# Running sums of a chunked scan: from a product with ones to rows in device memory read back by all partitions

## The chip, the cores and the metric

The kernel runs on one core of a Trainium2 chip. The metric is device time in microseconds. TensorE (PE), VectorE (DVE), ScalarE (ACT), GpSimd (POOL) and SyncE (SP) each work through a queue of their own, in order; "PEld" is PE's loading of weights, which overlaps its matmuls. SP here only issues DMA transfers.

## What the reference computes

Two layers on x of 2 batches, 512 tokens, 256 features, all in float32. Layer 0 is a Mamba-2 block (a chunked selective scan) whose result is multiplied by the silu of a mixture of 8 experts (2 of 8 per token). Layer 1 is attention with 32 heads over 8 key heads, multiplied by the silu of a layer with signs for weights. What matters here is the scan of layer 0:

```python
log_a = A_c * dt_c
cum_log_a = jnp.cumsum(log_a, axis=2)
log_diff = cum_log_a[:, :, :, None, :] - cum_log_a[:, :, None, :, :]
L = jnp.exp(jnp.where(causal, log_diff, -jnp.inf))
...
decay_to_end = jnp.exp(chunk_log_decay[:, :, None, :] - cum_log_a)
decay_from_start = jnp.exp(cum_log_a).reshape(batch, n_chunks, Q, G, Hg)
```

The running sum of the log decays is needed twice in each difference: as a number per token on the partitions, and as a row along the free dimension that is the same on all partitions.

## The kernel before

The scan is cut into 8 tiles of 128 tokens (t = 0 to 7; four per batch, i0 = 0 to 3) with 4 heads each. For all tiles at once `running_sums` makes `cum`, tokens on partitions, by a product of the triangle `upper` with the log decays `la` (L456), and DVE copies it out of PSUM (L458).

The sums along the free dimension are made tile by tile. `spread` (L466) has DVE multiply the triangle with the tile's log decays, giving `rl` of 128x512 (L470). `decays` (L474) has PE multiply ones with `rl` (L481): every partition then holds all running sums of the tile, 4 heads by 128, in one PSUM bank. From there ACT takes the exponential `ec` (L483), and DVE takes the four differences `L` (L490) and `dte` (L493). PE also turns the tile's inputs (L487, four transposes), which DVE scales to `xdt` (L497). `weighed`, `outputs` and `passed` finish the tile later; they use `ec`, `L`, `xdt`.

Around the scan stand the experts. One expert is `expert_turned` (PE transposes, L606, and DVE's copy to `xgT`, L608), three calls of `expert_hidden` (PE products at L624, ACT's silu at L633, DVE's multiplication at L636 to L641), and `expert_end` (PE at L649, ACT's scaling at L586, POOL's scatter at L587). Rows that overflow an expert go through `rests`: POOL gathers their weights as "piece" tiles (L575), and PE multiplies by them at L719 and L751. The order of all this is written out by hand from L771 to L1084 under a manual schedule: each engine, SP included, gets its instructions in the order of these lines.

SP's queue in this stretch holds the experts' weights: after each `expert_end` come `last_weights_of` (`wp`, 768 KB, L377, which must wait until PE has ended the expert) and `weights_of` (`w`, 1024 and 384 KB, L370 and L371). The part of the order around the second batch's first tile reads:

```python
        expert_end(3)
        last_weights_of(4)
        weights_of(5)
        convolved(1, 3)
        spread(1, 0)
        expert_hidden(4, 2)
        decays(1, 0)
        expert_turned(5)
```

The tag `rl` has two buffers, so `rl` of tile t uses again the buffer of tile t - 2. PSUM has two groups of four banks, "A" for the experts and "B" for the scan.

Of the kernel before, what the change touches and what calls it, by code (L numbers as in the profile page):

```python
# [8 lines left out]
F32 = mybir.dt.float32  # L9
AF = mybir.ActivationFunctionType  # L10
ALU = mybir.AluOpType
AX = mybir.AxisListType

P = 128
B, T, C = 2, 512, 256
NT = B * T // P
TPB = T // P
KC = C // P
DI, NH = 512, 4
# [32 lines left out]
def fused_kernel(  # L52
# [16 lines left out]
    nc = tc.nc  # L69
    V, S, G, PE = nc.vector, nc.scalar, nc.gpsimd, nc.tensor  # L70
# [9 lines left out]
    dram = ctx.enter_context(tc.tile_pool(name="dram", bufs=1, space=bass.MemoryType.DRAM))  # L80
# [7 lines left out]
    def bank_b():  # L88
        return psum.tile([P, 512], F32, tag="B", name="bank_b")
# [4 lines left out]
    def bank(width=512):  # L94

        if not later:
            return bank_b()
        i = turns[0] % 8
        turns[0] += 1
        written[i] = max(written[i], width)  # L100
        return later[i]
# [35 lines left out]
    ones = const.tile([P, P], F32, tag="ones", name="ones")  # L137
    G.memset(ones, 1.0)

    upper = const.tile([P, P], F32, tag="upper", name="upper")  # L140
# [40 lines left out]
           allow_small_or_imprecise_dtypes=True)  # L181
    rows = dram.tile([B * T, C], F32, tag="rows", name="rows")
    chosen = dram.tile([2 * B * T, C], F32, tag="chosen", name="chosen")

    first = const.tile([P, NT, E], F32, tag="first", name="first")
    for e in range(E):
# [99 lines left out]
    def narrow(weights, source):  # L286

        ps = bank_b()
        for g in range(GROUPS):
            for k in range(KC):  # L290
                PE.matmul(ps[g * QUARTER : (g + 1) * QUARTER, : 2 * P], lhsT=weights(k),
                          rhs=source(g, k), start=(k == 0), stop=(k == KC - 1))
        return ps
# [56 lines left out]
    def wide(name, t):  # L350
        return mw.tile([P, NH, P], F32, tag=name, name=f"{name}{t}")

    def lent(tag, name, *shape):

        n = 1
        for d in shape:
            n *= d
        flat = mw.tile([P, NH, P], F32, tag=tag, name=name).rearrange("p h n -> p (h n)")[:, :n]
        if len(shape) == 1:
            return flat  # L360
        names = "abc"[: len(shape)]
        return flat.rearrange(f"p ({' '.join(names)}) -> p {' '.join(names)}",
                              **dict(zip(names, shape)))
# [59 lines left out]
    la = mem.tile([P, NT, NH], F32, tag="la", name="la")  # L423
# [29 lines left out]
    def running_sums():  # L453
# [3 lines left out]
                  start=True, stop=True)  # L457
        V.tensor_copy(cum.rearrange("p t h -> p (t h)"), ps[:, : NT * NH])  # L458

    def heads(ap):  # L460
        return ap.rearrange("p (h n) -> p h n", h=NH)


    states, parts = [None] * B, {}

    def spread(b, i0):  # L466

        t = b * TPB + i0
        rl = wide("rl", t)
        V.tensor_tensor(rl, upper.unsqueeze(1).to_broadcast([P, NH, P]),  # L470
                        la[:, t, :].unsqueeze(2).to_broadcast([P, NH, P]), ALU.mult)
        parts[t] = rl

    def decays(b, i0):  # L474

        t = b * TPB + i0
        ti = slice(i0 * P, (i0 + 1) * P)

        cps = bank_b()
        cumb = heads(cps)  # L480
        PE.matmul(cps, lhsT=ones, rhs=parts[t].rearrange("p h n -> p (h n)"), start=True, stop=True)  # L481
        ec = wide("ec", t)
        S.activation(ec, cumb, AF.Exp)  # L483

        xps = bank_b()
        for h in range(NH):
            PE.transpose(xps[:, h * P : (h + 1) * P], ssmT[b][:, h, ti], ident)  # L487
        L = wide("L", t)
        for h in range(NH):
            V.scalar_tensor_tensor(L[:, h, :], cumb[:, h, :], cum[:, t, h : h + 1], negm,  # L490
                                   ALU.subtract, ALU.add)
        dte = mw.tile([P, NH], F32, tag="dte", name=f"dte{t}")
        V.tensor_tensor(dte, cumb[:, :, P - 1], cum[:, t, :], ALU.subtract)  # L493
        S.activation(L, L, AF.Exp)
        S.activation(dte, dte, AF.Exp)
        xdt = wide("xdt", t)
        V.tensor_tensor(xdt, heads(xps), dt3[:, t, :].unsqueeze(2).to_broadcast([P, NH, P]),  # L497
                        ALU.mult)
        parts[t] = ec, L, xdt, dte
# [18 lines left out]
    def outputs(b, i0):  # L518

        t = b * TPB + i0  # L520
        ec, L, xdt, cs, xe = parts[t]
        state = states[b]
        if xe is not None:
            sps = bank_b()
            PE.matmul(sps, lhsT=Btok[:, t, :], rhs=xe.rearrange("p h n -> p (h n)"),
                      start=True, stop=True)
            new = mw.tile([P, NH, P], F32, tag=f"state{b}", name=f"state{t}")
            if state is None:
                V.tensor_copy(new, heads(sps))
            else:  # L530
                for h in range(NH):
                    V.scalar_tensor_tensor(new[:, h, :], state[:, h, :], ec[:, h, P - 1 : P],
                                           heads(sps)[:, h, :], ALU.mult, ALU.add)
            states[b] = new
        yps = bank_b()
        for h in range(NH):
            y = yps[:, h * P : (h + 1) * P]
            PE.matmul(y, lhsT=xdt[:, h, :], rhs=L[:, h, :], start=True, stop=state is None)
            if state is not None:
                PE.matmul(y, lhsT=state[:, h, :], rhs=cs[:, h, :], start=False, stop=True)  # L540
        parts[t] = yps
# [229 lines left out]
    with tc.manual_schedule():  # L771

        ps = bank_b()
# [11 lines left out]
        for t in range(TPB + 1, NT):  # L785
# [16 lines left out]
        ps = narrow(lambda k: gw[:, k, :],  # L802
                    lambda g, k: xT[:, k, g * 2 * P : (g + 1) * 2 * P])
# [14 lines left out]
        ps = narrow(lambda k: w_in[:, k, o_dt - DI : o_dt - DI + QUARTER],  # L818
                    lambda g, k: hT[g // 2][:, k, g % 2 * 2 * P : (g % 2 + 1) * 2 * P])
# [8 lines left out]
        ps = bank_b()  # L828
        PE.matmul(ps[:, : counted[1]], lhsT=upper, rhs=both[:, 1:].rearrange("p t e -> p (t e)"),
                  start=True, stop=False)  # L830
        PE.matmul(ps[:, : counted[1]], lhsT=ones,
                  rhs=sums[0][:, 3 : 4 + NT].rearrange("p t e -> p (t e)"),
                  start=False, stop=True)
# [67 lines left out]
        ps = bank_b()  # L901
        for t in range(NT):
            for n in range(2):
                PE.matmul(ps[n * HALF : (n + 1) * HALF, :P], lhsT=vals[n][:, t, :],
                          rhs=ohs[n, t // TPB][:, t % TPB, :], start=(t == 0), stop=(t == NT - 1))
# [6 lines left out]
        ps = bank_b()  # L912
# [21 lines left out]
        expert_turned(0)  # L934
        expert_slots(1)
        spread(0, 0)
        gates(0, (3,))

# [22 lines left out]
        next(few)  # L961
        expert_hidden(1, 0)
        decays(0, 0)
        spread(0, 1)
        expert_end(0)
        last_weights_of(1)
        weights_of(2)
        weighed(0, 0)
        decays(0, 1)
        expert_hidden(1, 2)  # L970
        expert_turned(2)
        expert_slots(3)
        weighed(0, 1)
        within(0, 0)
        spread(0, 2)
        expert_hidden(1, 4)
        expert_hidden(2, 0)
        within(0, 1)
        decays(0, 2)
        expert_end(1)  # L980
        last_weights_of(2)
# [439 lines left out]
    with tc.manual_schedule():  # L1421
        prev = done = None
        for n, (b, c) in enumerate(work):
# [35 lines left out]
            if done is not None and done[1] == PAIRS - 1:  # L1459
                kept(*done)  # L1460
                done = None
                for i in range(TPB):
                    ps = bank(C)
# [15 lines left out]
        for i in range(2, TPB):  # L1479
            ps = bank(C)  # L1480
# [89 lines left out]
```

## Time and profile before

| | us |
|---|---|
| median of 3 runs | 630.01 (629.48 to 631.99) |
| the profiled execution | 630.42 |
| its span | 627.7 |
| scan and experts, within the span | about 39 to 235 |
| layer 1, mostly attention | about 235 to 627.7 |

The granted clock of TensorE was 0.997 of full speed in the profiled execution. The page of the profile lists for each engine its busy time, the span in 40 equal slices (15.7 us each; a digit is tenths of busy time), the DMA queues, the chain of work that ended last, and the costliest groups of instructions. A timeline lists, for one engine, start, duration, line, operation, output and inputs, count, and in brackets the idle time ahead of it with what ended it. Windows list the busy time of each engine in each stretch, with the number of instructions, then the granted clock, the share of the 16 DMA engines and GB/s.

### The profile page before, as it was taken

What the parts mean: (1) busy time and instruction counts of PE and PEld (TensorE: products, weight loads), DVE (VectorE), ACT (ScalarE), POOL (GpSimd) and SP (SyncE); (2) the same over time, 40 slices, a digit from 0 to 9 for tenths busy, and PEclk for the clock granted to TensorE, in tenths of its full rate; (3) what the DMA queues carried; (4) which work ended last, traced back from release to release, by engine and by line L of the source; (5) the groups of instructions that cost most, each with busy time, mean ns of one, the idle gap of its engine ahead of it and who ended that gap; (6) DMA issues with size and microseconds to landing.
All of it is one profiled execution on the core that took longest, in us unless ns stands there. A gap on an engine that the chain in (4) does not pass through costs nothing.

```text
span 627.7 us, 11001 instructions
## 1 busy us (share of the span) xinstructions
PE 602.3 (96%) x3847; PEld 410.7 (65%) x3847; DVE 424.9 (68%) x1349; ACT 352.4 (56%) x913; POOL 279.5 (45%) x312
## 2 busy tenths in 40 slices
PE   8989999999998988899889999999999999999997
PEld 6458888777766855365455565666866566666676
DVE  7687764464444238799997789986159888898411
ACT  3533333133331432879788677887048999999610
POOL 3021421364663131575635546565025776666700
PEclk9999999999999999999999999999999999999999
DMA  7810641675865253000000000400000000000000
GB/s 224 280 34 17 235 159 35 223 228 185 288 199 186 72 180 137 2 2 2 1 2 2 1 1 2 135 2 2 18 17 2 2 2 1 3 2 1 2 8 26
DMA packets 24988, 45.74 MB, mean 73 GB/s; under 512 B 2621, under 2 KB 12607, under 8 KB 24928
## 3 DMA queue, kind: packets, MB, share of 16 engines
q1 hardware_dynamic: 19840, 30.71, 14.3%
q0 software_dynamic: 4512, 13.77, 7.1%
q8 instruction: 31, 0.51, 0.3%
q10 hardware_dynamic: 576, 0.52, 0.2%
q14 instruction: 29, 0.24, 0.1%
HBM read 40.80 MB, written 4.33 MB: 72 GB/s over the span
## 4 chain that ended last, share of the span: by engine, by line
PE 46%; DVE 15%; ACT 3%; issue 2%; POOL 2%; ACTq 0%; DVEq 0%; POOLq 0%
PE bank L1302 9%; PE bank L1294 8%; PE bank L1175 7%; PE bank L1243 7%; PE bank L1282 7%; DVE pr L1256 5%; PE bank_a L649 2%; ACT pr L1262 2%; PE bank L1192 1%; POOL pr L1270 1%; DVE sw_q L1165 1%; PE bank_a L260 1%; PE bank_a L624 1%; DVE q L1166 1%; PE bank L1154 1%
## 5 line engine op out<-in xcount | busy, mean ns | idle before, releaser
L1270 POOL TENSOR_SCALAR pr<-pr,den 128x128 f32<-128x128 f32 (+2 forms) x192 | 193.5, 1024 | 146.4 <-DVE den L1435 146.4
L1262 ACT ACTIVATE pr<-pr,nmax 128x128 f32<-128x128 f32 (+3 forms) x256 | 142.2, 562 | 44.4 <-DVE nmax L1256 43.6
L1256 DVE CUSTOM_DVE_ANT_0 pr<-bank,cmask 128x128 f32<-128x128 f32 (+3 forms) x256 | 109.7, 484 | 12.7 <-PE bank L1243 9.2
L1283 ACT COPY pt<-bank 128x384 f32<-128x384 f32 (+1 forms) x192 | 82.4, 526 | 12.6 <-PE bank L1282 12.6
L1282 PEld LDWEIGHTS bank<-ident,pr 128*128 128x128 f32 x640 | 71.6, 141 | 21.6 <-issue 14.4
L1282 PE MATMUL bank<-ident,pr 128*128 128x128 f32 x640 | 75.6, 273 | 4.0 <-DVE oT L1419 3.5
L624 PE MATMUL bank_a<-xgT,w 128*128 128x256 f32 x352 | 79.5, 379 | 0.0
L1294 PE MATMUL bank<-pt,v 128*64 128x384 f32 (+3 forms) x512 | 77.0, 439 | 1.4 <-ACT pt L1283 1.4
L1243 PE MATMUL bank<-kT,q 64*64 64x128 f32 (+7 forms) x1024 | 69.9, 410 | 2.5 <-ACT v L1194 2.5
L624 PEld LDWEIGHTS bank_a<-xgT,w 128*128 128x128 f32 x352 | 65.6, 190 | 9.2 <-issue 1.0
L1294 PEld LDWEIGHTS bank<-pt,v 128*64 128x64 f32 x512 | 35.6, 136 | 45.5 <-issue 22.2
L1175 PE MATMUL bank<-x1T,w_q 128*128 128x512 f32 x124 | 61.5, 618 | 0.0
L1302 PE MATMUL bank<-w_o,oT 128*128 128x256 f32 x256 | 56.1, 380 | 0.6 <-DVE oT L1416 0.6
L1302 PEld LDWEIGHTS bank<-w_o,oT 128*128 128x128 f32 x256 | 48.3, 190 | 7.7 <-DVE oT L1416 0.8
L1262 ACT ACTIVATION_READ_ACCUMULATOR pr<-pr,nmax 128x1 f32 x256 | 50.3, 197 | 0.0
L1243 PEld LDWEIGHTS bank<-kT,q 64*64 64x64 f32 x1024 | 38.0, 133 | 16.2 <-issue 5.1
L575 POOL DMA_INDIRECT piece<-in_moe,wrow x36 | 37.4, 1040 | 21.7 <-issue 9.5
L1175 PEld LDWEIGHTS bank<-x1T,w_q 128*128 128x128 f32 x124 | 21.0, 189 | 37.0 <-issue 27.0
L587 POOL DMA_INDIRECT chosen<-o,dest x16 | 16.3, 1016 | 63.9 <-ACT o L586 37.2
L649 PE MATMUL bank_a<-wp,hid 128*128 128x256 f32 x192 | 43.1, 380 | 0.4 <-PEq L1072 0.3
L575 POOL DMA_INDIRECT xg<-rows,tok x16 | 17.0, 1065 | 54.2 <-DVE res L924 31.5
L649 PEld LDWEIGHTS bank_a<-wp,hid 128*128 128x128 f32 x192 | 35.9, 190 | 6.3 <-issue 1.7
(277 smaller groups left out, 793.7 us busy)
## 6 DMA issues: line engine op xcount, KB each, us to landing
w<-in_moe SPq DMA_DIRECT2D x8, 1024.0 KB, 11.8
wp<-in_moe SPq DMA_DIRECT2D x8, 768.0 KB, 4.2
w<-in_moe SPq DMA_DIRECT2D x8, 384.0 KB, 8.7
w_q<-in_wq SPq DMA_DIRECT2D x2, 1024.0 KB
w_o<-in_wo SPq DMA_DIRECT2D x2, 1024.0 KB
rows<-xn SPq DMA_DIRECT2D x4, 256.0 KB, 2.2
xn<-chosen SPq DMA_DIRECT2D x4, 256.0 KB, 2.6
y<-chosen SPq DMA_DIRECT2D x4, 256.0 KB, 3.8
```

What stands on the lines that cost most here:

```text
L575: G.indirect_dma_start(out=buf, out_offset=None, in_=src[:, :], in_offset=bass.IndirectOffsetOnAxis(ap=at, axis=0), bounds_check=src.shape ...
L624: PE.matmul(ps[:, i * OWN : (i + 1) * OWN], lhsT=w[:, a : a + P], rhs=xgT[:, k * OWN : (k + 1) * OWN], start=(k == 0), stop=(k == KC - 1))
L649: PE.matmul(ps[:, :C], lhsT=hid[j // 2][:, a : a + P], rhs=wp[:, j * C : (j + 1) * C], start=(j == 0), stop=(j == 5))
L1175: PE.matmul(ps, lhsT=w[:, k, n * P : (n + 1) * P], rhs=x1T[:, k, batch(b)], start=(k == 0), stop=(k == KC - 1))
L1243: PE.matmul(pss[hh][to, a : a + full], lhsT=q[half, n * HD : (n + 1) * HD], rhs=kT[b][half, m, :full], start=True, stop=True)
L1256: V.tensor_tensor_reduce(w["pr"][hh][:, span(i)], w["ps"][i][hh], cmask[:, i & 1, T - (i + 1) * P :], -1.0, 3.0e38, ALU.add, ALU.min, w["n ...
L1262: S.activation(x, x, AF.Exp, scale=-1.0, bias=w["nmax"][hh][:, i : i + 1], accum_out=sum_of(w, i, hh))
L1270: eng.tensor_scalar(x, x, sum_of(w, i, hh), None, ALU.mult)
L1282: PE.transpose(ps[:, col : col + P], pr[hh][:, at : at + P], ident)
L1283: S.copy(pts[hh][:, bank_at[n] : bank_at[n] + widths[n]], ps[:, : widths[n]])
L1294: PE.matmul(pv[hh * HD : (hh + 1) * HD, j * P :], lhsT=v_sb[b][:, j, g * HD : (g + 1) * HD], rhs=pts[hh][:, at : at + w], start=(j == 0), ...
L1302: PE.matmul(ps[:, :C], lhsT=oTs[b][:, c, i * P : (i + 1) * P], rhs=made["w_o"][c // 8][:, c % 8, :], start=(c == 0), stop=(c == PAIRS - 1))
```

## The change

The sums by row are made once for all tiles, by a second product with the operands exchanged (32 rows, one for each tile and head, by 128 tokens), copied out of the same PSUM bank by DVE, and written to device memory as `cum_rows` (16 KB). `spread` is no longer DVE's work: it is a DMA on SP that reads the tile's four rows (2 KB) to all 128 partitions (256 KB in SBUF). `decays` uses that tile in place of the PSUM bank. The places of the calls in the order stay as they were. In after.py the new product is L461, its copy L464, the write L465, the loads L477, the exponential `ec` L489 and the differences `L` L496.

```diff
+    cum_rows = dram.tile([NT * NH, P], F32, tag="cum_rows", name="cum_rows")
...
+        PE.matmul(ps[: NT * NH, P : 2 * P], lhsT=la.rearrange("p t h -> p (t h)"), rhs=upper,
+                  start=True, stop=True)
+        by_row = lent("yg", "by_row", P)[: NT * NH]
+        V.tensor_copy(by_row, ps[: NT * NH, P : 2 * P])
+        nc.sync.dma_start(cum_rows[:, :], by_row)
...
     def spread(b, i0):
 
         t = b * TPB + i0
-        rl = wide("rl", t)
-        V.tensor_tensor(rl, upper.unsqueeze(1).to_broadcast([P, NH, P]),
-                        la[:, t, :].unsqueeze(2).to_broadcast([P, NH, P]), ALU.mult)
-        parts[t] = rl
+        cumb = wide("rl", t)
+        nc.sync.dma_start(cumb.rearrange("p h n -> p (h n)"),
+                          cum_rows[t * NH : (t + 1) * NH, :].rearrange("a n -> (a n)")
+                          .partition_broadcast(P))
+        parts[t] = cumb
...
     def decays(b, i0):
...
-        cps = bank_b()
-        cumb = heads(cps)
-        PE.matmul(cps, lhsT=ones, rhs=parts[t].rearrange("p h n -> p (h n)"), start=True, stop=True)
+        cumb = parts[t]
         ec = wide("ec", t)
         S.activation(ec, cumb, AF.Exp)
```

## The prediction, made before the changed kernel had run

> **What bounds the kernel now.** I read the page first: TensorE (PE) is busy 96% of the span, the granted clock is full in every slice, and no other engine passes 68%. Then the slices. The scan and the experts that stand around it lie between about 39 and 235 us, where the DMA row is busy too.
>
> ```profile
> PE 602.3 (96%) x3847; PEld 410.7 (65%) x3847; DVE 424.9 (68%) x1349; ACT 352.4 (56%) x913; POOL 279.5 (45%) x312
> ...
> DMA  7810641675865253000000000400000000000000
> ```
>
> Then the same stretch in windows of 1 us. From 60 to 174 us PE never idles (the sum for 84 to 108 us is 24.00 of 24). So time taken off PE's queue is gained, and a wait that reaches PE is lost, unless something else was already late at the next meeting point. That something is the gather of "piece" tiles by GpSimd (POOL), below.
>
> **What is removed.** The product at L481, its operand at L470 (VectorE, DVE, 0.68 us, eight times). The row of L481 by line, and the place of its first pair in PE's timeline:
>
> ```profile
> L481 PE MATMUL bank_b<-rl,ones x16: 592/592/697, 57.5 to 208.8; 128*128 128x512 f32 x16
> ...
> 57.48 1.02 PE L481 MATMUL bank_b<-rl,ones 128*128 128x512 f32 x2
> 58.34 0.60 PE L487 MATMUL bank_b<-ident,ssmT 128*128 128x128 f32 x4
> ```
>
> Matmuls overlap, so I don't take 592 ns but the distance to the next start: 58.34 - 57.48 = 0.86 us for a pair. The eight pairs read 0.86, 0.86, 0.86, 0.85, 0.86, 0.96, 0.96, 0.86: 7.07 us. Ahead of the seventh pair PE also idles 0.97 us for L470 (it starts at 176.55); that wait goes, and the transposes behind need only old data. Together **-8.04**. The DVE time saved (5.5 us) is worth nothing by itself: PE, not DVE, is the queue without gaps. ScalarE (ACT) and DVE also stop taking turns on the bank of L481 (DVE waited 17.3 us for L483, six times), off PE's path as well; so is what reading SBUF instead of PSUM does to their 0.34 and 0.60 us.
>
> **What is added at about 40 us.** A second product (after.py L461) of 128 columns in the bank that holds the first. In the built program's list of waits it holds a wait of its own for DVE, for the count that the copy of the first product (L458) reaches. That copy is queued on DVE behind a whole convolution (timelines of PE, then DVE, of before):
>
> ```profile
> 39.45 0.38 PE L456 MATMUL bank_b<-la,upper 128*128 128x32 f32 x2 [1.66 <-DVE la L449]
> 39.67 1.96 PE L260 MATMUL bank_a<-hT,w_z 128*128 128x512 f32 x4
> ...
> 39.80 2.33 DVE L402 SCALAR_TENSOR_TENSOR cv<-pad,sm,cv 128x512 f32<-128x512 f32 x3
> 42.04 0.18 DVE L458 COPY cum<-bank_b 128x32 f32<-128x32 f32 x1
> ```
>
> PE now goes on at 39.67. After the change it stands until 42.22, plus 0.14 from DVE's end to PE's start (as from la, 39.12 + 0.19, to 39.45), plus 0.22 for the product (the distance L456 to L260): 42.58, 2.91 us later. Behind it in PE's queue are two gate projections and the transposes of the first expert's tokens; the latter now wait for a gather and take 0.87 us (41.47 to 42.34) instead of 0.44, so 0.43 is absorbed. **+2.48**. Bounds: 0 if the wait were already met, which the times exclude unless DVE is 2.5 us earlier; 2.9 if nothing is absorbed. The second copy (L464) and xgT behind it on DVE stay ahead of PE: xgT would end near 45.6, PE needs it at 46.5.
>
> On this wait the Trainium skill, "PSUM — Partial Sum Buffer", section "PSUM bank collisions raise a hardware error", says that two engines must not touch one bank and quadrant at once, whatever the columns. By it the wait can't be left out and PE pays the 2.48; a rule by bytes alone would give 0 here, as the two products use different columns.
>
> **The write and the eight loads.** The 16 KB write leaves SyncE (SP) near 43 us. SP's writes of now, rows<-xn and out_x<-y, land 2.2 and 1.7 us after issue. Loads 0 and 1 go right behind, by about 48 us, and are needed from 59.6 us (L483): hidden. The others stand on SP in program order behind weights, whose issue waits for PE to end an expert (L649). What counts is the time from that issue to the use:
>
> - Load 2 (SP near 65.7): DMA is saturated until 73.6, so landing near 74.5; needed near 80. Hidden.
> - Load 3 (near 88.3): saturated until 95; landing near 96.4; ACT reaches its use at 97.5. Hidden by 1 us; if late, ACT and DVE have some 10 us before PE needs them.
> - Load 5 goes with load 4 and is needed at 160; load 6 (near 159) lands near 168.5, needed at 176; load 7 (near 185) lands near 193, needed at 208. Hidden.
> - **Load 4** (near 138.6) is not.
>
> ```profile
> 138.05 0.51 SPq L371 DMA_DIRECT2D w<-in_moe  x1
> ...
> w<-in_moe SPq DMA_DIRECT2D x1, 384.0 KB, 8.7
> ...
> 145.00:146.00 1.00, 1.00 (x12) 0.26 (x8) 0.12 (x1) 0.83 (x2) 0.00 (x0) 1.00 0.87 291
> 146.00:147.00 1.00, 1.00 (x11) 0.37 (x4) 0.72 (x2) 0.15 (x1) 0.00 (x0) 1.00 0.14 50
> ```
>
> The first two rows are SP's issue of the last weights ahead of it and their landing: 138.05 + 8.7 = 146.75. The window rows end in DMA share and GB/s; they show the transfers ending there. At the 393 GB/s of 143 to 145 us 256 KB more takes 0.65-0.7: 147.4. The use is L490 on DVE, now at 142.05:
>
> ```profile
> 142.05 1.12 DVE L490 SCALAR_TENSOR_TENSOR L<-bank_b,cum,negm 128x128 f32<-128x128 f32 x4 [0.73 <-ACT ec L483]
> 143.10 0.15 DVE L493 TENSOR_TENSOR dte<-bank_b,cum 128x4 f32<-128x4 f32 x1
> 143.17 0.68 DVE L497 TENSOR_TENSOR xdt<-bank_b,dt 128x512 f32<-128x512 f32 x1
> 143.76 0.68 DVE L608 COPY xgT<-bank_a 128x512 f32<-128x512 f32 x1
> ...
> 146.96 3.62 PE L624 MATMUL bank_a<-xgT,w 128*128 128x256 f32 x16
> ```
>
> Behind L490 on DVE is xgT of expert 5 (L608), and PE's products of that expert wait for it. xgT starts 1.71 us after L490, so 149.11, ends 149.8, PE starts near 149.95. Without the wait PE would be there at 146.96 - 0.86 = 146.10. **+3.85**. ACT's silu behind its own wait (L483) comes back by 151 and stays ahead of PE. Bounds: 0 if the load overtakes the weights; above, the slowest 256 KB rows of the page take 3.8 us from issue to landing (y<-chosen), which behind the queue makes +7.0. I take 3.85, the rate of the queue it stands in, as the nearest row.
>
> The Trainium skill, "DMA: Bandwidth & Descriptors", section "Anatomy of one DMA — SWDGE (gpsimd) path", gives 2.0 us plus bytes over 436 GB/s for one transfer on the other path, an estimate of 2.6 us here. Paid in full behind the weights it would make this wait 5.8 instead of 3.85 and the forecast 631.4; no run here shows it.
>
> **Where the gain meets another wait.** Pieces 4 and 5 are gathered by POOL from 160.30 to 170.88, counted from the end of expert 4, and PE's L719 at 173.59 already takes some 0.5 us more than its 384 columns need (1.99 us against 1.92 for 512). The 0.96 of the sixth pair lies between: PE arrives earlier and waits longer. **+0.96** (bounds 0 and 0.96). Likewise the last piece:
>
> ```profile
> 200.47 0.62 PE L751 MATMUL bank_b<-piece,hrT 128*32 128x256 f32 x2 [0.80 <-DMA piece<-in_moe,wrow]
> 201.80 1.05 PE L751 MATMUL bank_b<-piece,hrT 128*32 128x256 f32 x10 [0.72 <-DMA piece<-in_moe,wrow]
> ```
>
> Its gather follows a scatter on POOL that took 7.0 us (185.79 to 192.79; 3.2 at 155.76) while DMA was full. The weights come 1.9 us earlier against it, load 7 adds 0.65. I take **+0.2**; bounds -1.5 (the waits vanish) and +1.93 (all of the seventh pair is given back).
>
> **Sum:** -8.04 + 2.48 + 3.85 + 0.96 + 0.2 = -0.55. The profiled execution took 630.42 (span 627.7 and 2.7 around it), so 629.9; against the median 630.01, **629.5**. After 235 us nothing changes but the start.
>
> **Rivals.** (1) Load 4 isn't late: the DMA engines might serve it between packets of the weights. Against it: the last weights land just as the transfers end, so the queue is served in order. Then 3.85 more goes: 625.6. (2) Slower: the load itself is slow, because 128 readers ask for the same 2 KB. Load 4 then holds DVE, and PE behind it, for each us more. It ends slower by 0.5% (3.15 us) once the transfer takes 0.65 + 3.7 = 4.35 us (60 GB/s); at 49 GB/s, an eighth of the queue's rate, 5.3 us, +4.7: 634.1. For it: no row shows a load of one row by all partitions. Against it: rows of 2 KB run at 390 GB/s here. (3) The products stay in some form: the built program has none of L481's, so no chance.
>
> **Numbers.** Forecast 0.56 (its own range 627.5 to 632.5), rival 1 0.14, rival 2 0.30, which takes in other late loads. About 0.5% (3.15 us) is what a measurement of this kernel can tell from none: faster 0.14, within 0.56, slower 0.30. Range 625.5 to 634.5: rival 1, the bounds above (629.5 + 3.15 + 1.7 = 634.35) and the near part of rival 2.
>
> **What would show it.** Right: a PE wait for DVE (cum) of about 2.7 us near 40; DVE waiting at the fifth L (after.py L496) some 5 us for the load; PE waiting near 4 us for xgT behind it; L719 and L751 waiting longer for pieces. Wrong: no gap ahead of expert 5; loads 2, 3, 6 late as well; or landings 4 us and more behind the weights.

## The result, and the profile after

The changed kernel takes 636.52 us (median of 4 runs, 634.79 to 637.58); before, beside it, 629.80 (629.48 to 631.99). The ratio is 1.0082, 95% interval 1.0058 to 1.0106: slower by 0.8%, where 629.5 and no difference were forecast. The profiled execution took 636.41 us with a span of 634.5, 6.8 us longer than the span of before.

The page of the changed kernel, its rows of PE's busy time and of the granted clock:

```profile
PE 601.8 (95%) x3833; PEld 410.1 (65%) x3833; DVE 419.9 (66%) x1342; ACT 352.9 (56%) x913; POOL 278.1 (44%) x312
...
PEclk9979999998999998999999999999999999999999
```

PE runs 14 matmuls fewer and is busy almost as long (601.8 beside 602.3). The clock row says why: it is no longer full in the third, the tenth and the sixteenth slice (32 to 48, 143 to 159 and 238 to 254 us). The first two are the places of the two waits that the forecast counted. The third, at half from 248.6 to 255.4, lies around a wait of 3.60 us ahead of the transposes of xn (249.85). It adds nothing that is seen in the total: from the decays of (1,3) to the end both kernels take as long (418.3 and 418.4 us). PE's timeline at the first place:

```profile
39.32 0.38 PE L457 MATMUL bank_b<-la,upper 128*128 128x32 f32 x2 [1.66 <-DVE la L450]
42.15 0.63 PE L461 MATMUL bank_b<-upper,la 128*32 128x128 f32 x2 [2.45 <-DVE cum L459]
42.72 3.78 PE L261 MATMUL bank_a<-hT,w_z 128*128 128x512 f32 x4
46.29 1.05 PE L612 MATMUL bank_a<-ident,xg 128*128 128x128 f32 x4
47.15 1.92 PE L261 MATMUL bank_a<-hT,w_z 128*128 128x512 f32 x4
```

The wait is the forecast one, in place and length: the second product (L461) stands 2.45 us for DVE's copy and starts at 42.15. But what follows is slow: the gate projection (L261) takes 3.57 us to the next start and the transposes 0.86; the same projection at 47.15, once the clock is back, takes 1.75. The windows give the reason, here and for the second place further down (length, busy time of PE, PEld, DVE, ACT and POOL, then **PEclk, the granted clock**, DMA share, GB/s):

```profile
40.00:41.00 1.00, 0.00 (x0) 0.00 (x0) 0.96 (x2) 0.00 (x0) 0.00 (x0) 0.69 0.32 90
...
42.00:43.00 1.00, 0.85 (x3) 0.47 (x4) 0.27 (x2) 0.97 (x2) 0.00 (x0) 0.50 0.00 0
...
46.00:47.00 1.00, 1.00 (x5) 0.71 (x4) 0.00 (x0) 0.46 (x1) 0.00 (x0) 0.50 0.87 211
47.00:48.00 1.00, 1.00 (x4) 0.57 (x3) 0.62 (x2) 0.13 (x1) 0.59 (x1) 0.90 0.65 240
...
153.00:154.00 1.00, 1.00 (x4) 0.82 (x3) 0.04 (x1) 0.99 (x3) 0.47 (x1) 0.51 0.64 172
...
156.00:157.00 1.00, 1.00 (x5) 0.84 (x4) 0.04 (x1) 0.60 (x1) 0.00 (x0) 0.78 0.00 0
```

While PE stands, the clock falls to 0.50 (at 40.4), and it comes back only at 47.2: PE works 5.1 us at half speed after its wait. The first products of the first expert start at 48.90 instead of 44.05: 4.85 us lost. The two rows of before with which the two places are compared, from PE's timeline:

```profile
44.05 6.21 PE L624 MATMUL bank_a<-xgT,w 128*128 128x256 f32 x28
...
150.42 1.02 PE L525 MATMUL bank_b<-xe,Btok 128*128 128x512 f32 x2
```

The second place of the changed kernel, in the timelines of DVE, then PE:

```profile
150.13 1.14 DVE L496 SCALAR_TENSOR_TENSOR L<-rl,cum,negm 128x128 f32<-128x128 f32 x4 [6.46 <-DMA rl<-cum_rows]
...
151.89 0.68 DVE L614 COPY xgT<-bank_a 128x512 f32<-128x512 f32 x1
```
```profile
148.12 0.49 PE L513 MATMUL bank_b<-BC 128*128 128x128 f32 x2
152.62 5.41 PE L630 MATMUL bank_a<-xgT,w 128*128 128x256 f32 x16 [4.01 <-DVE xgT L614]
157.86 1.02 PE L531 MATMUL bank_b<-xe,Btok 128*128 128x512 f32 x2
```

This is the forecast chain link by link: load 4 holds DVE at the fifth L, xgT of expert 5 stands behind it, PE waits 4.01 us. PE was 1.48 us late at L513 (148.12 against 146.64) and is 5.66 late at L630. Then its 16 matmuls take 5.24 us to the next start; before they took 3.46 (146.96 to 150.42). The clock is 0.50 from 153.0 to 156.4, and PE leaves 7.44 us late.

Loads 0 and 1 show what a load costs by itself. They are what the DMA columns of the windows at 46 and 47 us above hold (211 and 240 GB/s); the window before them has 70 GB/s, the one behind them 4. Both, 512 KB, move between 45.5 and 48 us: about 1.25 us each. That is twice the 0.65 that the forecast took from the rate of the weights, and far below the 4.35 from which rival 2 would have been slower by 0.5%.

### The profile page after: what moved, and what is told of

It is laid out like the page before. It is cut to its first block, busy times and chain, and to the rows that moved or that the text cites. A ratio compares the mean times of both kernels' runs of the same rounds, so it can differ in the third digit from the quotient of the medians.

```text
span 634.5 us, 10977 instructions
## 1 busy us (share of the span) xinstructions
PE 601.8 (95%) x3833; PEld 410.1 (65%) x3833; DVE 419.9 (66%) x1342; ACT 352.9 (56%) x913; POOL 278.1 (44%) x312
## 4 chain that ended last, share of the span: by engine, by line
PE 51%; DVE 11%; ACT 2%; issue 1%; POOL 1%; DVEq 0%; POOLq 0%
PE bank L1300 10%; PE bank L1308 9%; PE bank L1181 8%; PE bank L1249 8%; PE bank L1288 8%; DVE pr L1262 4%; PE bank_a L655 2%; PE bank L1198 1%; POOL pr L1276 1%; PE bank_a L261 1%; PE bank L1160 1%; PE bank_a L630 1%; DVE sw_q L1171 1%; PE bank_b L1181 1%; DVE q L1172 1%
## 5 line engine op out<-in xcount | busy, mean ns | idle before, releaser
L630 PE MATMUL bank_a<-xgT,w 128*128 128x256 f32 x352 | 81.7, 386 | 4.8 <-DVE xgT L614 4.0
L630 PEld LDWEIGHTS bank_a<-xgT,w 128*128 128x128 f32 x352 | 66.7, 193 | 15.3 <-DVE xgT L614 4.2
L1300 PEld LDWEIGHTS bank<-pt,v 128*64 128x64 f32 x512 | 35.4, 136 | 45.7 <-issue 22.5
```

Of the source, the lines that this page charges most:

```text
L630: PE.matmul(ps[:, i * OWN : (i + 1) * OWN], lhsT=w[:, a : a + P], rhs=xgT[:, k * OWN : (k + 1) * OWN], start=(k == 0), stop=(k == KC - 1))
L1300: PE.matmul(pv[hh * HD : (hh + 1) * HD, j * P :], lhsT=v_sb[b][:, j, g * HD : (g + 1) * HD], rhs=pts[hh][:, at : at + w], start=(j == 0), ...
```

## The experiments

The table follows PE by the start of the transposes (bank_b<-ident,ssmT) in the decays of four chunks, and by the span, in the profiled execution of each kernel. The ratio is that of all its runs to the runs of before on the same chip.

| kernel | (0,0) | (1,0) | (1,1) | (1,3) | span | ratio, 95% interval |
|---|---|---|---|---|---|---|
| before | 58.34 | 141.22 | 160.26 | 209.27 | 627.7 | 1 |
| after | 62.29 | 142.71 | 166.74 | 216.18 | 634.5 | 1.0082 [1.0058, 1.0106] |
| e1_own_bank | 57.35 | 137.81 | 160.82 | 210.96 | 629.1 | 1.0030 [1.0007, 1.0054] |
| e2_early_load | 62.08 | 142.48 | 160.56 | 211.48 | 628.8 | 0.9988 [0.9965, 1.0011] |
| e3_both | 57.49 | 137.98 | 156.27 | 207.93 | 625.5 | 0.9903 [0.9871, 0.9936] |
| e4_kept_busy | 60.07 | 142.04 | 165.24 | 218.28 | 635.7 | 1.0073 [1.0044, 1.0102] |
| e5_loads_alone | 58.14 | 141.03 | 160.06 | 211.56 | 630.2 | 1.0014 [0.9991, 1.0037] |
| e6_no_last_loads | 57.33 | 137.52 | 155.59 | 204.46 | 622.3 | 0.9926 [0.9903, 0.9948] |
| e7_act_queue | 62.39 | 143.05 | 162.48 | 212.51 | 631.1 | 1.0021 [1.0001, 1.0041] |
| e8_first_wait | 63.34 | 146.67 | 165.70 | 218.71 | 635.7 | 1.0084 [1.0045, 1.0123] |
| e9_first_wait_busy | 60.82 | 144.07 | 163.10 | 212.31 | 630.8 | 1.0049 [1.0029, 1.0069] |
| e10_both_busy | 58.90 | 139.39 | 157.46 | 206.43 | 624.6 | 0.9934 [0.9909, 0.9959] |
| e11_after_again | 61.45 | 141.85 | 165.82 | 215.97 | 633.7 | 1.0079 [1.0049, 1.0108] |

Theory W+C: the two waits, each with a clock at half speed behind it. Rivals: the waits alone (W), the loads' traffic (D), a slow load (S). A fourth, P, comes up with e5: the last pieces end late there whatever PE gains before.

### e1_own_bank: the first wait taken away

```
-        PE.matmul(ps[: NT * NH, P : 2 * P], lhsT=la.rearrange("p t h -> p (t h)"), rhs=upper,
+        pr = bank_b()
+        PE.matmul(pr[: NT * NH, :P], lhsT=la.rearrange("p t h -> p (t h)"), rhs=upper,
```

> The changed kernel (636.5 us) with the second product in a PSUM bank of its own, so that it no longer waits for the copy of the first. Theory W+C (two waits of TensorE, and after each the granted clock at half for some us): the 2.5 us gap at 42 goes, and with it the half clock from 40.7 to 47; the first expert starts near 44.2 instead of 48.9; 636.5 - 4.8 = 631.7. Rival W (the waits cost what they last, the clock is there for another reason): the half clock stays somewhere near 41 to 47 and 636.5 - 2.6 = 633.9 comes out. Theory D (the traffic of the loads is the cost): 636.

In its trace the second product starts at 39.64, the clock stays at 1.00 from 36 to 60 us, and the first expert starts at 43.96 instead of 48.90. So the 4.85 us belong to this bank and to nothing else of the change. Of the total, 5 per mille (3.3 us) go, less than W+C expected and nearer to W's number, although the place looks as W+C has it. In this trace the gain holds to the end (a span of 629.1 us against 634.5), so the median gains less than the trace. Over the 12 executions of e1 the span goes from 628.0 to 634.1 us as the mean granted clock goes from 0.995 to 0.987, which points at other falls of the clock. The wait ahead of expert 5 is still there (2.99 us), with a half clock from 147.3 to 150.8.

### e2_early_load: the second wait taken away

```
         last_weights_of(4)
+        spread(1, 0)
         weights_of(5)
         convolved(1, 3)
-        spread(1, 0)
```

> The changed kernel with load 4 alone moved in SyncE's order, from behind expert 5's weights to behind expert 4's (about 25 us earlier); its data, size and use stay. W+C: the 4.0 us gap ahead of expert 5 goes and so does the half clock behind it; 636.5 - 4.1 - 1.8 = 630.6. Rival W: 632.4. Rival S (the load is slow because all partitions read one row): the load is still late or others are; above 634.

No wait and no half clock ahead of expert 5 (its products start at 148.22 and take 3.46 us). The first wait is there as before. 9.4 per mille go, 5.9 us: the 4.18 of the wait and the 1.78 of the clock that the trace of the changed kernel shows. Rival W expected 4.1.

### e3_both: both edits

> Both edits: second product in its own bank, load 4 early. W+C: the two savings add, 636.5 - 4.8 - 5.9 = 625.8, faster than the kernel before by 4. Rival W: 629.8, as before. Theory D (contention of the loads with weights and pieces costs the gain): 629 or more with waits for pieces between 175 and 203 us that are longer than in the changed kernel (2.0 us of DMA waits there).

626.54 us against 631.34 on its chip; the ratio over all runs is 0.9903, faster than before by 1.0% (0.6 to 1.3). Without the two waits the change does gain: 6.1 us by the ratio, 4.8 by the medians, of the 8.04 that were removed. This is the version to keep.

### e4_kept_busy: the waits stay, PE works through them

```
+    def busy(n):
+        ps = bank_b()
+        for _ in range(n):
+            PE.matmul(ps[:, :P], lhsT=ident, rhs=ident, start=True, stop=True)
...
+        busy(10)
         PE.matmul(ps[: NT * NH, P : 2 * P], lhsT=la.rearrange("p t h -> p (t h)"), rhs=upper,
...
         weighed(1, 0)
+        busy(18)
```

> The changed kernel with all its waits kept, but TensorE filled during the two with products of the identity that nobody reads: 10 pairs ahead of the second product, 18 pairs ahead of expert 5 (about 0.22 us a pair). The filler takes no wait away. W+C: the granted clock stays full at both places; 636.5 - 2.4 - 1.8 = 632.3. Rival W: 636.5 or a little more.

The total didn't follow: 1.0073, hardly under the 1.0082 of the change, which is near what rival W expected. At both places the clock stays at 1.00 and PE gets what the clock had taken: the first expert starts at 46.68 instead of 48.90 (2.22), and the products of expert 5 take 3.56 us instead of 5.24 (1.68). But then PE comes early to things that don't: at 77.26 it waits 1.76 us (0.21 for weights in the changed kernel; here the trace names DVE's yg, and the weights' transfers run until 76.5), load 4 still lands at 150.3, and ahead of the last pieces PE waits 0.94 and 1.80 us, with a new fall of the clock at 211.4. So the price of the clock is shown at the place, and not by this total.

### e5_loads_alone and e6_no_last_loads: is it the traffic of the loads?

e5 adds six loads to the kernel before; e6 leaves two out of e3, so its chunks (1,2) and (1,3) work with the sums of two others. Of e6 the main lines:

```
+        if t in (1, 2, 3, 5, 6, 7):
+            nc.sync.dma_start(used_rl[t - 1].rearrange("p h n -> p (h n)"),
+                              rope[0, 0, : NH * P].partition_broadcast(P))
```
```
+        if t >= NT - 2:
+            parts[t] = loaded[t - 2]
+            return
```

> The kernel before, with six added loads of 256 KB (one row of an input read by all partitions) issued on SP where the changed kernel issues loads 1, 2, 3, 5, 6 and 7; they land in a tile that nobody reads any more, and the products stay. It asks whether the loads' traffic alone is what makes the stretch from the decays of (1,2) to those of (1,3) longer: 31.8 us before, 33.3 in the changed kernel, 34.8 in e3_both. Theory D (traffic): the stretch grows by 1.5 us or more, and the kernel takes 1.5 to 3 us more than before. Rival P (the chain of pieces on POOL is what ends late there, and PE's earlier arrival is given back as waiting): the stretch stays within 0.5 us of 31.8 and the total within 1 us of before.

> e3_both without loads 6 and 7: chunks (1,2) and (1,3) use the row sums that were loaded for (1,0) and (1,1), so those two loads are left out and the output is not the reference's there. Theory D (traffic of the last two loads): the stretch from the decays of (1,2) to those of (1,3) goes from 34.8 us back to about 32, and the total from 626.5 to about 624. Rival P (the chain of pieces on POOL): the stretch stays between 34 and 35.5 and the total within 1 us of e3_both's ratio to before, 0.990.

e5 takes 1.0014 with 1 inside its interval. Its stretch from (1,2) to (1,3) is 35.65 us (175.91 to 211.56), as theory D had it, so by that number D holds and by the total P does. e6 speaks against D in the total: without the two loads it is at 0.9926, not under the 0.9903 of e3, so their traffic costs nothing that is measured. Its stretch, 32.94 us (171.52 to 204.46), is again nearer to D's 32 than to P's 34 to 35.5. The stretch was a poor choice: it starts behind a wait of 0.97 us (for rl) that some traces have and others don't. From (1,1) to (1,3) it is clearer. It takes 49.01 us before, with products; 48.87 in e6 and 49.44 after, without; 49.21 in e9, with products and no loads; 48.97 in e10, with loads and no products. In e2, e3, e4, e5, e7 and e8 it is 50.0 to 53.0, and those six are the traces in which the clock is at half somewhere between 200 and 215. (e1 and e11 have 50.1 without a fall.) So PE's saving hardly shortens this stretch, if at all. What PE waits for in it, in the timeline of e3:

```profile
198.41 0.62 PE L758 MATMUL bank_b<-piece,hrT 128*32 128x256 f32 x2 [1.03 <-DMA piece<-in_moe,wrow]
199.85 1.65 PE L758 MATMUL bank_b<-piece,hrT 128*32 128x256 f32 x10 [0.81 <-DMA piece<-in_moe,wrow]
```

The last pieces, gathered by POOL, as before the change. In the changed kernel the products on pieces and the idle time ahead of them take 9.94 us of this stretch, 7.81 before. That the pieces set the stretch is read from such rows; a run with faster gathers wasn't made.

### e7_act_queue: the load in another queue

```
+        queue = nc.scalar if t == TPB else nc.sync
-        nc.sync.dma_start(cumb.rearrange("p h n -> p (h n)"),
+        queue.dma_start(cumb.rearrange("p h n -> p (h n)"),
```

> The changed kernel with one edit: load 4 is issued by ACT instead of SP, so that it no longer stands behind the weights of expert 5. Queue theory: it then lands within 5 us of its issue, well ahead of 142 us, DVE waits for it under 1 us, there is no wait of PE over 1 us ahead of expert 5 and no half clock at 150 to 157; the ratio to before falls from 1.008 to about that of e2_early_load, 0.999. Rival S (the load itself is slow, 128 readers of one row, as in rival 2 of the forecast): it still takes 9 us from issue to landing, and as the issue comes little earlier the wait ahead of expert 5 stays above 2 us; ratio 1.005 or more.

The DMA issues of e7 from 139 to 142 us (KB, median us from issue to landing):

```profile
w<-in_moe SPq DMA_DIRECT2D x1, 384.0 KB, 10.5
rl<-cum_rows ACTq DMA_DIRECT2D x1, 256.0 KB, 5.9
rl<-cum_rows SPq DMA_DIRECT2D x1, 256.0 KB, 10.5
```

Load 4 takes 5.9 us in ACT's queue; in SP's, behind the weights, it took 9.1 in the changed kernel, and load 5, as large and issued 1.6 us after load 4 here, takes 10.5. So the order in the queue is the larger part of its lateness. It still lands at 145.7, not well ahead of 142, with 2.2 MB of weights beside it; DVE waits 1.7 us and PE 1.12 (both over what was expected), PE this time, by the trace, for DVE's hid (L646), which waits for ACT's silu, and without a fall of the clock there. The total, 1.0021, lies midway between the two theories. That the rest of the lateness is the sharing of the DMA engines with the weights isn't shown. Loads 0 and 1, with little beside them, take 3.5 us from issue to landing (median of the two).

The Trainium skill, "DMA: Bandwidth & Descriptors", says in its section "Issuing engines are not separate DMA queues" that issuing from several engines saves only the time to issue, as all transfers run on the same 16 DMA engines, and in "Queues, rings and completion order" that SP and ACT each have a row of rings between which each DMA engine takes turns. The runs side with the second: 3.2 us less for load 4 than in SP's queue, and 4.6 less than for load 5 beside it.

### e8_first_wait and e9_first_wait_busy: the first wait alone, without and with its half clock

e8 is the kernel before with L461, the copy and the write, and nothing else; e9 has busy(10) ahead of L461 as well.

> The kernel before, with only the second product in the first one's bank, its copy and the write to device memory added; products of ones and the triangle stay, and no load is made. It prices the first wait by itself. W+C (the wait of 2.5 us and a clock at half speed behind it): PE idles about 2.5 us near 40, the clock is 0.50 to about 47, the decays of (0,0) come 4.9 us later than before (63.2), those of (1,0) still 4.5 to 5 later, and the kernel takes 3.3 to 5.4 us more: ratio 1.005 to 1.0085. Rival W (the wait alone): the decays of (0,0) come 2.5 us later, ratio 1.004.

> e8_first_wait (the kernel before with only the second product, its copy and the write) with ten small products on identities put ahead of the second product, in a bank of their own, so that PE works through the wait instead of standing. It takes the half clock away and leaves the wait. W+C: the clock stays at 1.00 from 39 to 50 us, the decays of (0,0) come at about 61.1 instead of 63.3, and of the 8.4 per mille that e8 costs 3 to 4 go: ratio 1.004 to 1.006; less comes back if the weights that land at 77 us, or the pieces, are then late, as in e4_kept_busy. Rival W (the clock is only a sign of the idling and costs nothing): the decays of (0,0) stay at 63.3, ratio 1.008.

e8 costs 8.4 per mille, 5.3 us, as much as the whole change: a product, a copy, a write, and a wait that was priced at 2.48. In e9 PE works from 39.62 on (fillers), and the second product starts as late (42.23; 42.15 in e8). From 44 to 45 us the clock is 0.50 in e8 and 1.00 in e9. The gate projection in PE's timeline of e8, then of e9:

```profile
42.71 3.78 PE L261 MATMUL bank_a<-hT,w_z 128*128 128x512 f32 x4
```
```profile
42.56 1.98 PE L261 MATMUL bank_a<-hT,w_z 128*128 128x512 f32 x4
```

With the clock at 1.00 the same four matmuls take 1.83 us to the next start instead of 3.58, and the decays of (0,0) come at 60.82 instead of 63.34: 2.52 us come back though PE has more to do. That is the price of the clock, by itself; rival W is out. In the totals 3.5 per mille come back (2.2 us), as expected, but the two intervals overlap.

### e10_both_busy: does a better clock late in the stretch pay?

e3 with eight fillers ahead of the last pieces and nine ahead of the output projections of the second sequence.

```
+            if q == 0 and i == PIECES - 1:
+                busy(8)
...
+            if i0 == 0:
+                busy(9)
             projected_out(1, i0)
```

> e3_both with small products on identities in three more waits of PE: eight ahead of the last pieces of the remainder (PE waited 1.84 us in two parts there, and the clock fell from 200.4 to 203.7), and nine ahead of the output projections of the second sequence (2.06 us, clock at half to 234.9). If the falls there cost what they show, 1.7 us each, and don't come back elsewhere: ratio to before 0.985 (about 621.5 beside 631). If the falls only move to a later idle stretch (there are waits of 1.9 us near 241 and 252), or the waits simply are set by other engines: 0.989 to 0.991, as e3_both.

0.9934, its interval overlapping that of e3 (0.9871 to 0.9936): no gain is shown. The clock stays up at the two places. At the first that pays: from (1,1) to (1,3) PE takes 48.97 us instead of e3's 51.66. At the second it doesn't: PE waits 3.58 us instead of 1.89 ahead of the next transposes (of xn), which start as long after (1,3) as in e3 (33.44 and 33.51 us). And the clock falls at two others: from 40.8 to 44.3, after which (0,0) comes at 58.90 instead of e3's 57.49, and from 238.8 to 245.7. A window at the first, behind PE's wait of 1.66 us for la that ends at 39.20:

```profile
43.00:44.00 1.00, 1.00 (x4) 0.65 (x3) 0.44 (x1) 0.50 (x2) 0.42 (x1) 0.50 0.07 16
```

### e11_after_again: the change a second time

> The changed kernel once more, on the chip and beside the runs of before that e9 and e10 share, to have the three on one footing: ratio 1.006 to 1.0105, as in the first comparison. In its trace the two waits (2.45 us near 42, 4.0 us near 152) and the half clock behind each should be the same; which later waits (near 200, 232 and 250) let the clock fall may differ, if that depends on where the wait meets a clock that runs by itself.

1.0079: the result repeats. The waits are 2.44 and 4.16 us. The first half clock begins later and is shorter (42.3 to 45.7; 40.4 to 47.2 there), and (0,0) is 3.11 us late instead of 3.95: the wait has a fixed length, the fall behind it has not.

## Why the prediction was wrong, point by point

- **Products and the idle time for rl, -8.04: right.** From the decays of (0,3) to those of (1,0), where nothing else differs, PE takes 41.92 us instead of 42.78: the 0.86 of a pair. e3 realizes 4.8 to 6.1 of the 8.04.
- **The first wait, +2.48: place, cause and length right, price wrong; this is the step that failed.** The prediction read a wait as its own length and let PE go on at the rows of before, at full clock; the clock stood in its sum at nothing, without a reason. It cost 4.85 us at its place. 2.45 is the wait; the rest, 2.4, is that PE ran at half speed for 5.1 us after it. e8 and e9 show it.
- **Load 4, +3.85: the same.** Landing at 150.1, DVE's wait, xgT and PE's wait came as worked out (4.18 for 3.85; SP issued the weights ahead of it 2.34 later than before, and the load landed 2.7 later than the 147.4 of the forecast). The clock behind it took 1.78 more. From the decays of (1,0) to those of (1,1) PE takes 24.03 us instead of 19.04, with a pair of 0.96 removed: 5.95.
- **Given back at other waits, +0.96 and +0.2: too small.** From (1,1) to (1,3) two pairs and the 0.97 were removed, 2.79, and the stretch grew by 0.43 (49.01 to 49.44): 3.2 instead of 1.16, of which 2.1 are at products on pieces and the waits ahead of them. Another 0.97 is lost from (0,0) to (0,2), where 6.36 and 15.44 us stand against 6.70 and 15.85 with a pair removed from each; waits of 0.26 us for ScalarE's hid at 63.15 and 0.21 for weights at 77.92 are part of it.
- **The sum.** -8.04 + 4.85 + 5.95 + 3.2 + 0.97 = 6.93; from (1,3) to the end 0.1 comes off (418.3 us against 418.4). The spans differ by 6.8.
- **Loads 2, 3, 5, 6 and 7 hidden: right.** No wait for them reaches PE.
- **Rival 1 (load 4 not late): refuted** by the waits of DVE and ACT at 150. **Rival 2 (a slow load): refuted**; two loads moved in 2.5 us, where it needed 4.35 for one. Their 1.25 each, against the 0.65 of the forecast, is a small miss beside it. The slower case came, for a reason that was no rival. **Rival 3: excluded as said.**

The clock row of before had invited the mistake: full in all 40 slices. In windows of 1 us it is not. There too it stands at 0.50 from 232.6 to 236.0 us, behind a wait of PE of 2.19 us that ends at 232.50. The trace of before held that row for whoever asked what PE's idle stretches do to the clock.

The Trainium skill, "TensorE: Matmul & The Clock Gate", section "What's actually happening", describes this: PE's activity is judged in windows of 3.4 us that run by themselves, and after an idle one the clock is at half. The runs agree on the length: 153.0 to 156.4 is 3.4 us, and the longest falls, such as 40.4 to 47.2, are two of them. They differ on what must lie ahead: in the 3.4 us before the fall at 40.4 PE was not idle but busy for 0.32 of the time. For how long a gap is harmless, its section "Why this matters for your kernels" says that gaps of PE should not exceed about 3 us. By that rule each of the two waits at 40, 1.66 and 2.45 us, would have kept the clock, and the second would have cost its 2.45; the runs differ.

## What to carry to other kernels

Price a new wait of TensorE by its length and by the clock behind it: here a wait of 2.45 us cost 4.85, and one of 4.0 cost 5.95. Look at the granted clock in windows of 1 us around PE's idle stretches of the profile at hand, not at the page's slices. Before giving up a change like this one, look at what the waits hang on: a bank of its own and a load put ahead of the weights in its queue, two edits of one or two lines, turned +0.8% into -1.0% (-0.8% by the medians).

## What the runs showed of the hardware that was not expected

- **When the clock falls.** Counted over the 13 traces: the wait of 1.66 us near 38, where none of 2.45 follows it, dropped the clock in one of 8 (e10); the 1.66 and 2.45 together in 5 of 5; waits of 1.82 to 2.36 us for held, between 227 and 242, in 5 of 12; waits of 2.99 to 4.16 ahead of expert 5 in 3 of 3; waits of 2.92 to 3.60 ahead of the transposes of xn, between 237 and 252, in 8 of 8, and of 1.89 there in 2 of 5. One of 2.51 us at 254.8 in before dropped nothing.
- **What decides it is a grid, not the length alone.** In these traces the clock falls 30 times between 36 and 276 us. Each fall lasts 3.41 or 6.83 us, and within a trace all of them begin on one grid of 3.413 us. Of the steps of that grid at full clock, 862 in all, PE was busy for at most 0.40 of the time in 20, and a fall followed each of these; between 0.41 and 0.52 it followed 9 of 23, above that 1 of 819. The same wait of 2.19 us for held lies within one step in before (229.21 to 232.62, PE busy 1.22 us: a fall) and is divided between two in the changed kernel (234.92 to 238.33 and on to 241.75, PE busy 1.96 and 2.67 us: none). Where the grid lies differs from trace to trace, so a wait under about 3 us can cost its length in one execution and more in the next.
- **A fall that is taken away may come back elsewhere.** e4 and e10 each kept the clock up at two places and lost it at others. One such place can be followed. In the 5 traces with a fall behind the wait for held, PE waits 1.89 us ahead of the transposes of xn; in the 7 without, PE is done sooner, waits 2.92 to 3.60 us there, and the clock falls then. The transposes start 10.7 to 10.8 us after the first product on held in 10 of these 12 traces, with the fall and without (10.1 and 10.2 in the other two). So the half clock behind the wait for held costs nothing that is seen: the next step doesn't wait for PE there.
- **One row read by 128 partitions:** two loads of 256 KB moved in 2.5 us. One took 3.4 to 4.8 us from issue to landing near 45 us, with little beside it, 5.9 in ACT's queue beside weights, and 6.8 to 11.3 in SP's behind them.
